# Edge attention on a graph: clip and exps for two batches at once, messages a round later, and more column tiles

## The chip, the cores and the metric

The kernel runs on one core of one Trainium2 chip. The metric is the device time of one execution in microseconds. Engines are named as the profile names them: PE (TensorE: matmuls, and PEld for its weight loads), DVE (VectorE), ACT (ScalarE), POOL (GpSimd), SP (SyncE, which issues DMAs here).

## What is computed

A graph has N = 6250 nodes of 128 features and E = 206250 edges, sorted by the node they end in. Heads H = 8 of width 16. Cut to what matters:

```python
Qh, Kh, Vh = h @ WQ, h @ WK, h @ WV          # per node, as (N, 8, 16)
Eh = edge_attr @ WE                          # per edge
score = einsum('ehd,ehd,ehd->eh', Kh[src], Qh[dst], Eh) / sqrt(16)
score = exp(clip(score, -5, 5))
msg = Vh[src] * score[:, :, None]
wV, Z = segment_sum(msg, dst), segment_sum(score, dst)
out = layernorm(x + wV / (Z + 1e-6))
```

Each edge needs the K and V rows of its source node (a random node) and the Q row of its end node (neighbours in the sorted order).

## The kernel before, in words

**Tiles and batches.** 128 edges are a tile; there are 1612 tiles. A batch is four tiles (`B`), 401 of these, and five last ones of two or one tile (the last `TAIL` = 8 tiles), 406 batches in all. The main loop (L621) makes a round for each batch, plus three rounds that drain it.

**K and V rows.** For the first 12 batches (`XB`) POOL gathers rows of x itself and PE projects them (`project`, L440). Meanwhile `table` (L271) projects all nodes and writes the rows of K and V to a table in HBM. From batch 12 on, `gather` (L420) fetches rows of 256 numbers from that table with one indirect DMA for each tile (L429), issued by POOL, into one of `GB` = 12 buffers `kvrows`. In program order a gather stands `GLEAD` = 2 rounds ahead of its use, on POOL's own queue; from batch 18 on it also waits for the Q expansion of a batch `lag(b)` rounds back (L361: 12 rounds at first, one fewer every 40 batches, never under 3).

**Column tiles.** 163 batches have their fourth tile built without a gather: three batches in seven (`COLP = (7, 3)`), from batch 24 on. The columns of x for its 128 edges are copied one by one out of `xT_sb` into a tile `xcol`, at addresses that are loaded into registers first (L391). ACT copies `COLA` = 8 x 11 = 88 of them, one instruction each (L402); DVE copies `COLV` = 8 x 5 = 40, two to an instruction by an OR of two addresses (L399). "Runs" are eight columns with one register load: eight instructions on ACT, four on DVE. `columns` (L372) issues the runs that are due at a point of the round. PE then projects the tile (`project_columns`, L404, two rounds before the batch's turn), and ACT copies the result into the batch's `kvrows` (`place_columns`, L414).

**A round.** For batch b PE makes the edge projection `eps` and the expansion of Q rows `qps` (`stage_a`, L489). DVE multiplies for the batch before it, b - 1 (`stage_b`, L504): `kq` (L507), `kqe` (L510), the sum over each head `sc` (L513), the clip (L516). Then ACT takes the exp twice (`weigh`, L519): into the message tile (L523) and into `exp_p` in PSUM (L524). DVE makes the message of batch b - 2 (`messages`, L555), and PE adds batch b - 2 into its window of nodes with one matmul a tile against a one-hot matrix (`stage_c`, L562, `agg`). DVE builds the one-hot matrices for two batches at a time (`stage_0`, L462, and `stage_0t`, L474), so every other round. When a window of 16 tiles is complete, ACT copies it to one of `SUMS` = 9 buffers; `finish` (L541) adds windows to blocks of 256 nodes (`finps`), ACT copies these (`fin`, L550), and `layernorm` runs on DVE.

**What sets the order.** From batch 12 on the order on each engine is the program order (`manual_schedule`, L623). Each round of DVE is written out by hand (L653 to L673): kq, one-hot or column runs, `fill`, kqe, one-hot or column runs, `fill`, sc, message, column runs, `fill`, clip, `fill`. `fill` (L613) puts in one small instruction: a cast or difference of the next block of Q rows (`q_rows`, L302, whose matmul PE makes at the end of a round, L689), or one step of a layernorm. Column runs stand behind kq and kqe only in rounds without one-hots.

Of the kernel before, what the change touches and what calls it, by code (L numbers as in the profile page):

```python
# [9 lines left out]
F32 = mybir.dt.float32  # L10
# [4 lines left out]
ALU = mybir.AluOpType  # L15
AX = mybir.AxisListType

P = 128
N, E, D, H, DH = 6250, 206250, 128, 8, 16
NT = (E + P - 1) // P  # L20
EPAD = NT * P
B = 4
# [5 lines left out]
MW = D + H  # L28
# [8 lines left out]
LAST = NT - TAIL  # L37
# [12 lines left out]
QLOOK = 3  # L50
QREG = 16
COL0 = 24
COLP = (7, 3)
COLA = (8, 11)
COLV = (8, 5)
COLL = 8
RING = 4096
XCOLS = 4
SUMS = 9
XT_AT = RING + P  # L60
NB = (N + P - 1) // P

# [40 lines left out]
def edge_attention(ctx: ExitStack, tc: tile.TileContext, x, xT, srcT, srcC, dstT, dstB, dst0, bnd, lo, eaT,  # L103
                   wq, wkv, we, out, kv, qtab, qs, relD):
    nc = tc.nc
# [26 lines left out]
    batches = cut_batches()  # L132
# [8 lines left out]
    with ExitStack() as fast:  # L141
# [105 lines left out]
        psX = fast.enter_context(tc.tile_pool(name="psX", bufs=1, space=bass.MemoryType.PSUM))  # L247

        iota_p = psX.tile([P, HW], F32, name="iota_p")
        exp_p = psX.tile([P, B, H], F32, name="exp_p")  # L250
        nc.vector.tensor_copy(iota_p, iota_f[:, :HW])

        def pair_bank(i, name, shape):
# [88 lines left out]
            nc.sync.dma_start(rels[c][:, :n], relD.rearrange("j e -> (j e)")[None, c * RC * P:c * RC * P + n]  # L342
                              .to_broadcast([QROWS, n]))

        chunks, aggs, sums, st8, expanded = {}, {}, {}, {}, {}

        def load_chunk(c):
            if c in chunks or c * CH >= NT:
# [20 lines left out]

        addresses, fetched = {}, {}  # L370

        def columns(eng, b, share=1.0):  # L372

            size, runs = COLA if eng is nc.scalar else COLV
            first = 0 if eng is nc.scalar else COLA[0] * COLA[1]
            engine = mybir.EngineType.Activation if eng is nc.scalar else mybir.EngineType.DVE
            copy = eng.copy if eng is nc.scalar else eng.tensor_copy
            due = int((b - COL0 + COLL - 1 + share) * runs * COLP[1] / COLP[0] + 1e-6)
            total = len(col_batches) * runs
            while copied.get(engine, 0) < min(due, total):  # L380
                k, j = divmod(copied.get(engine, 0), runs)
                copied[engine] = copied.get(engine, 0) + 1
                if k not in col_tiles:
                    col_tiles[k] = wp.tile([P, P], F32, name="xcol", bufs=XCOLS)
                to, j = col_tiles[k].bitcast(U8), first + j * size
                known = addresses.setdefault(engine, [])
                while len(known) < 2 and fetched.get(engine, 0) < total:
                    kf, jf = divmod(fetched.get(engine, 0), runs)
                    fetched[engine] = fetched.get(engine, 0) + 1
                    jf = first + jf * size  # L390
                    known.append(nc.values_load_multi_w_load_instructions(  # L391
                        col_at[kf % col_half:kf % col_half + 1, kf // col_half, jf:jf + size], engines=(engine,),
                        min_val=XT_AT, max_val=XT_AT + 8 * (N - 1) + 4,
                        skip_runtime_bounds_check_because="edges name nodes")[1])
                at = known.pop(0)
                if eng is nc.vector:
                    for c in range(0, size, 2):
                        both = [xT_bytes[:, ds(a - XT_AT, 8)] for a in at[c:c + 2]]
                        eng.tensor_tensor(to[:, 4 * (j + c):4 * (j + c) + 8], *both, op=ALU.bitwise_or)  # L399
                    continue  # L400
                for c in range(size):
                    copy(to[:, 4 * (j + c):4 * (j + c) + 4], xT_bytes[:, ds(at[c] - XT_AT, 4)])  # L402
# [50 lines left out]

        def together(b):

            t0 = batches[b][0]
            n = len(batches[b])
            if n == B and b + 1 < nbat and len(batches[b + 1]) == B and t0 % (2 * B) == 0:
                return [b, b + 1]
            return [] if n == B and t0 % (2 * B) else [b]  # L460

        def stage_0(b):  # L462
            group = together(b)
# [40 lines left out]
        def stage_b(b):  # L504
            n, g, oh, pq, pe = st8[b]
            t0 = wp.tile([P, B, D], F32, name="kq", bufs=2)
            nc.vector.tensor_tensor(t0[:, :n], g[:, :n, :D], pq[:, :n], op=ALU.mult)  # L507
            yield
            t1 = wp.tile([P, B, D], F32, name="kqe", bufs=2)
            nc.vector.tensor_tensor(t1[:, :n], t0[:, :n], pe[:, :n], op=ALU.mult)  # L510
            yield
            sc = wp.tile([P, B, H], F32, name="sc")
            nc.vector.tensor_reduce(sc[:, :n], t1[:, :n].rearrange("p b (h d) -> p b h d", h=H),  # L513
                                    axis=AX.X, op=ALU.add)
            yield
            nc.vector.tensor_scalar(sc[:, :n], sc[:, :n], -20.0, 20.0, op0=ALU.max, op1=ALU.min)  # L516
            st8[b] = [n, g, oh, sc]

        def weigh(b):  # L519

            n, g, oh, sc = st8[b]
            m = wp.tile([P, B, MW], F32, name="msg")
            nc.scalar.activation(m[:, :n, D:], sc[:, :n], AF.Exp, scale=0.25)  # L523
            nc.scalar.activation(exp_p[:, :n], sc[:, :n], AF.Exp, scale=0.25)  # L524
            st8[b] = [n, g, oh, m]

        def windows(q):

# [24 lines left out]
            blocks_out.append(copied_out)  # L553

        def messages(b):  # L555
            n, g, oh, m = st8[b]
            nc.vector.tensor_tensor(  # L557
                m[:, :n, :D].rearrange("p b (h d) -> p b h d", h=H),
                g[:, :n, D:].rearrange("p b (h d) -> p b h d", h=H),
                exp_p[:, :n, :, None].to_broadcast([P, n, H, DH]), op=ALU.mult)  # L560

        def stage_c(b):  # L562
            n, g, oh, m = st8.pop(b)
            for i in range(n):
                t = batches[b][i]
                k, _ = window_of(t)
                q = t * N // NT // P
                if q % 2 == 0 and q < NB and q not in loaded_x:
                    loaded_x.add(q)
                    xbs[q] = load_x(nc, sp, x, q, min(2, NB - q))  # L570
                final = k == NT
                if k not in aggs:
                    aggs[k] = psA.tile([P, 1, MW], F32, name="agg")
                    if final:
                        add_windows(aggs[k][:, 0], QL, True, False)
                tail = t == NT - 1 or window_of(t + 1)[0] != k
                nc.tensor.matmul(aggs[k][:, 0], oh[0][:, oh[1] + i * P:oh[1] + i * P + P], m[:, i, :],  # L577
                                 start=not final and t % (QUAD * G) == 0, stop=tail)
                if tail and final:
                    norms.insert(0, layernorm(nc, sp, aggs.pop(k), xbs.pop(QL), out, QL, 1, stores))  # L580
                elif tail:
                    sums[k] = sp.tile([P, MW], F32, name="sum", bufs=SUMS)
                    nc.scalar.copy(sums[k], aggs.pop(k)[:, 0])
                    while len(finished) < QL // 2 and all(v <= k for v, _ in windows(2 * len(finished) + 1)):
                        ready.append(len(finished))
                        finished.append(k)
# [23 lines left out]
        nc.vector.tensor_scalar(col_at, col_at, 8, XT_AT + 4, op0=ALU.mult, op1=ALU.add)  # L610
        second = col_at[:, :, COLA[0] * COLA[1]:].rearrange("p h (c s) -> p h c s", s=2)[:, :, :, 1]
        nc.vector.tensor_scalar(second, second, 4, None, op0=ALU.subtract)
        def fill():  # L613

            if qwork:
                build_q(0, False)
            elif norms and (not late or late.pop()) and next(norms[0], None) is None:
                norms.pop(0)

        held, late = [], []  # L620
        for b in range(nbat + 3):  # L621
            if b >= XB and not manual:
                manual.append(fast.enter_context(tc.manual_schedule()))  # L623
            held += [(b + SLAG, store) for store in stores]
# [29 lines left out]
            next(steps, None)  # L654
            if b + AHEAD < nbat and together(b + AHEAD):
                stage_0(b + AHEAD)
            elif b < nbat:
                columns(nc.vector, b, 0.5)
            fill()
            next(steps, None)  # L660
            if b + AHEAD < nbat and together(b + AHEAD):
                stage_0t(b + AHEAD)
            elif b < nbat:
                columns(nc.vector, b, 1.0)
            fill()
            next(steps, None)
            if 0 <= b - 2 < nbat:
                messages(b - 2)
            if b < nbat:
                columns(nc.vector, b)  # L670
            fill()
            next(steps, None)
            fill()  # L673
# [4 lines left out]
                blocks_out.pop(0)()  # L678
            if b < nbat:
                columns(nc.scalar, b)  # L680
            if 0 <= b - 2 < nbat:
                stage_c(b - 2)
            if b < nbat:
                project_columns(b + GLEAD)
                build_q(q_built(min(NJ - 1, batches[b][0] // WT + QLOOK + 2)), True)
                if not qwork and len(built) < q_built(
                        min(NJ - 1, batches[min(nbat - 1, b + 3)][0] // WT + QLOOK + 2)):
                    qwork.append(q_rows(len(built)))
                    next(qwork[0])  # L689
            if b == min(60, nbat):  # L690
                count_inside()
            if b == min(80, nbat + 1):
# [160 lines left out]
```

## Time and profile before

| | |
|---|---|
| median of 3 runs | 1854.44 us (1854.39 to 1854.63) |
| profiled execution | 1852.51 us, span of its profile 1850.7 us |
| mean granted TensorE clock | 0.918 |
| DMA | 378.38 MB, mean 204 GB/s |
| HBM read, written | 360.30 MB, 14.81 MB |

Times are microseconds, unless marked ns. In a group's row stand the line, the engine, the operation, the tiles written and read, the count, then the busy time and the mean ns of one instruction, then the idle time of the engine just before them and who ended most of it. "issue" is time in which an engine waited for nothing that the profile shows. In a table of stretches each engine has its busy time and, in brackets, the number of its instructions; behind them stand the granted clock, the DMA share and GB/s. In a table of waits stand the waiter, who released it, total us, times, and the longest. In the order of time a row has the start, the length and the count of the instructions merged. An instruction's length runs to its last write, and the next one of the engine starts before that, so what an instruction takes of its engine is read from start to start.

### The profile page before, as it was taken

To read this page: it belongs to the slowest core of one execution; us is meant where nothing else is said; L and a number is where in the kernel's file an instruction comes from. 1 tells how busy PE (TensorE), PEld (TensorE's weight loads), DVE (VectorE), ACT (ScalarE), POOL (GpSimd) and SP (SyncE) were. 2 spreads that over 40 slices of the span, in tenths; PEclk is the share of its full clock that TensorE was granted. 3 is DMA by queue.
4 is the path that set the end of the run, shared out by engine and by line. 5 is a ranking of instruction groups with operands and counts; after the bars stand their busy time and mean duration, and the time that the engine had idled before them with its cause. 6 is when DMAs were issued, how large, how long until landed. Compare 5 with 4: busy or idle time off the path is not lost.

```text
span 1850.7 us, 47948 instructions
## 1 busy us (share of the span) xinstructions
PE 1306.9 (71%) x9104; PEld 1134.8 (61%) x9104; DVE 1655.5 (89%) x6514; ACT 1626.7 (88%) x15519; POOL 1385.6 (75%) x1456
## 2 busy tenths in 40 slices
PE   6887767667677676667776676766766677667666
PEld 4776656566566565566665565655666667656555
DVE  5579999999998999999998898989998899898987
ACT  2439899899999999999999899999899899999983
POOL 6777777777777777777777777777777777777774
PEclk7998899899998989999899998999898988898998
DMA  9776667767766776767767677667776686667762
GB/s 283 231 230 194 195 204 230 204 184 213 223 192 192 221 207 200 225 196 208 216 196 207 188 204 220 195 187 224 209 207 182 194 236 187 197 188 229 216 190 76
DMA packets 171226, 378.38 MB, mean 204 GB/s; under 512 B 58622, under 2 KB 84556, under 8 KB 170918
## 3 DMA queue, kind: packets, MB, share of 16 engines
q0 software_dynamic: 68768, 186.80, 35.1%
q1 hardware_dynamic: 101010, 187.38, 33.9%
q14 instruction: 234, 1.92, 0.3%
q8 instruction: 74, 1.21, 0.3%
q10 hardware_dynamic: 1140, 1.06, 0.2%
HBM read 360.30 MB, written 14.81 MB: 203 GB/s over the span
## 4 chain that ended last, share of the span: by engine, by line
DVE 38%; DMA 15%; PE 14%; ACT 12%; issue 8%; POOL 6%; DVEq 4%; ACTq 2%; SPq 0%; POOLq 0%
DMA kvrows<-kv,src 13%; ACT xcol L402 10%; DVE xcol L399 7%; DVE kqe L510 7%; DVE kq L507 6%; POOL kvrows L429 6%; DVE sc L513 6%; PE eps L497 5%; DVEq L391 4%; PE agg L577 4%; DVE msg L557 3%; DVE onehot L469 3%; DVE onehotT L482 2%; ACTq L391 2%; PE kvps L451 1%
## 5 line engine op out<-in xcount | busy, mean ns | idle before, releaser
L429 POOL DMA_INDIRECT kvrows<-kv,src x1401 | 1338.0, 955 | 427.4 <-issue 318.7
L402 ACT COPY xcol<-xT_sb 128x4 uint8 x14344 | 1447.0, 191 | 52.1 <-issue 45.3
L497 PE MATMUL eps<-we_sb,ea 128*128 128x128 f32 x3224 | 499.6, 303 | 416.4 <-DVE kqe L510 243.7
L497 PEld LDWEIGHTS eps<-we_sb,ea 128*128 128x128 f32 x3224 | 435.3, 209 | 510.5 <-issue 351.4
L577 PE MATMUL agg<-msg,onehot 128*128 128x136 f32 x3224 | 533.2, 313 | 89.5 <-DVE msg L557 82.8
L577 PEld LDWEIGHTS agg<-msg,onehot 128*128 128x128 f32 x3224 | 454.4, 211 | 142.2 <-DVE msg L557 126.8
L507 DVE TENSOR_TENSOR kq<-kvrows,qps 128x512 f32<-128x512 f32 x406 | 275.7, 679 | 82.6 <-DMA kvrows<-kv,src 33.8
L399 DVE TENSOR_TENSOR xcol<-xT_sb 128x8 uint8 x3260 | 312.9, 162 | 26.8 <-issue 21.1
L557 DVE TENSOR_TENSOR msg<-kvrows,exp_p 128x512 f32<-128x512 f32 x406 | 273.1, 673 | 7.9 <-ACT exp_p L524 7.9
L510 DVE TENSOR_TENSOR kqe<-kq,eps 128x512 f32<-128x512 f32 x406 | 273.9, 675 | 3.0 <-PE eps L497 2.6
L513 DVE TENSOR_REDUCE sc<-kqe 128x32 f32<-128x512 f32 x406 | 272.2, 670 | 0.7
L500 PE MATMUL qps<-qw,onehotT 126*128 126x128 bf16 x1612 | 169.5, 230 | 0.0
L523 ACT ACTIVATE msg<-sc 128x32 f32<-128x32 f32 x406 | 92.5, 228 | 78.9 <-DVE sc L516 65.3
L500 PEld LDWEIGHTS <-onehotT 126*128 126x128 bf16 x1612 | 135.0, 104 | 8.6
L469 DVE TENSOR_TENSOR onehot<-iota_p,dst_sb 128x512 f32<-128x512 f32 (+2 forms) x206 | 138.2, 672 | 2.0 <-PE agg L577 2.0
L411 PE MATMUL colkv<-wkv_sb,xcol 128*128 128x256 f32 x326 | 108.0, 416 | 0.0
L482 DVE TENSOR_SCALAR onehotT<-relb,node 126x1024 bf16<-126x1024 bf16 (+2 forms) x206 | 102.7, 499 | 3.3 <-DMA relb<-relD 1.8
L516 DVE TENSOR_SCALAR sc<-sc 128x32 f32<-128x32 f32 x406 | 81.2, 200 | 0.3
L524 ACT ACTIVATE exp_p<-sc 128x32 f32<-128x32 f32 x406 | 73.6, 181 | 0.0
L429 POOL DMA_INDIRECT kvrows<-x,src x48 | 46.6, 971 | 20.5 <-issue 11.6
L418 ACT COPY kvrows<-colkv 128x256 f32<-128x256 f32 x163 | 58.9, 361 | 1.4 <-PE colkv L411 1.3
L411 PEld LDWEIGHTS colkv<-wkv_sb,xcol 128*128 128x128 f32 x326 | 56.9, 215 | 0.0
(76 smaller groups left out, 536.3 us busy)
## 6 DMA issues: line engine op xcount, KB each, us to landing
ea<-eaT SPq DMA_DIRECT2D x201, 512.0 KB
relb<-relD SPq DMA_DIRECT2D x100, 504.0 KB
kvrows<-kv,src POOLq DMA_INDIRECT x1401
qw<-qs SPq DMA_DIRECT2D x202, 31.5 KB
kv<-kvst SPq DMA_DIRECT2D x12, 512.0 KB
qs<-qst SPq DMA_DIRECT2D x48, 96.0 KB
xst<-xT SPq DMA_DIRECT2D x12, 256.0 KB
xb<-x SPq DMA_DIRECT2D x24, 128.0 KB
```

Source lines behind the costliest of these rows:

```text
L399: eng.tensor_tensor(to[:, 4 * (j + c):4 * (j + c) + 8], *both, op=ALU.bitwise_or)
L402: copy(to[:, 4 * (j + c):4 * (j + c) + 4], xT_bytes[:, ds(at[c] - XT_AT, 4)])
L411: nc.tensor.matmul(pk, col_tiles.pop(k), wkv_sb, start=True, stop=True)
L429: ins = nc.gpsimd.indirect_dma_start(out=g[:k, i, :f], out_offset=None, in_=rows, in_offset=bass.IndirectOffsetOnAxis(ap=src_col(t)[:k], a ...
L469: nc.vector.tensor_tensor(tl[:, HW:].rearrange("p (t n) -> p t n", n=P)[:, :n, :HW], iota_p[:, None, :].to_broadcast([P, n, HW]), rel[:, t ...
L497: nc.tensor.matmul(pe[:, i, :], ea[:, i * P:i * P + P], we_sb, start=True, stop=True)
L500: expanded[b] = nc.tensor.matmul(pq[:, i, :], ohT[:, i * P:i * P + P], loaded[t0 // WT], start=True, stop=True)
L507: nc.vector.tensor_tensor(t0[:, :n], g[:, :n, :D], pq[:, :n], op=ALU.mult)
L510: nc.vector.tensor_tensor(t1[:, :n], t0[:, :n], pe[:, :n], op=ALU.mult)
L513: nc.vector.tensor_reduce(sc[:, :n], t1[:, :n].rearrange("p b (h d) -> p b h d", h=H), axis=AX.X, op=ALU.add)
L557: nc.vector.tensor_tensor(m[:, :n, :D].rearrange("p b (h d) -> p b h d", h=H), g[:, :n, D:].rearrange("p b (h d) -> p b h d", h=H), exp_p[ ...
L577: nc.tensor.matmul(aggs[k][:, 0], oh[0][:, oh[1] + i * P:oh[1] + i * P + P], m[:, i, :], start=not final and t % (QUAD * G) == 0, stop=tail)
```

## The change

- `COLP` goes to (13, 6): six batches in 13 have a column tile. `COLA` is 8 x 10, `COLV` 8 x 6: ACT copies 80 columns of a tile, DVE 48. `SUMS` goes to 8.
- `columns` takes a bound `most`. DVE calls it at three places in every round with a bound of one run: behind kq (and a one-hot), behind kqe (and a one-hot), and behind the message. Before, it stood behind kq and kqe only in rounds without one-hots, and behind the message with no bound.
- Batches are paired (`together`, `group_of`): `sc`, the message tile and `exp_p` hold two batches. The sum over heads of each batch writes its half; the clip comes once, with the second; `weigh` takes both exps once, for the pair.
- `messages` and `stage_c` come for batch b - 3 in round b, where they came for b - 2; the loop has one round more.
- `fresh`: after the matmul of a block of Q rows, three calls of `fill` are counted down, the third of which makes the first cast.

```diff
-COLP = (7, 3)
-COLA = (8, 11)
-COLV = (8, 5)
+COLP = (13, 6)
+COLA = (8, 10)
+COLV = (8, 6)
...
-SUMS = 9
+SUMS = 8
...
-        exp_p = psX.tile([P, B, H], F32, name="exp_p")
+        exp_p = psX.tile([P, 2 * B, H], F32, name="exp_p")
...
-        def columns(eng, b, share=1.0):
+        def columns(eng, b, share=1.0, most=99):
...
-            while copied.get(engine, 0) < min(due, total):
+            while copied.get(engine, 0) < min(due, total) and most:
+                most -= 1
...
-            t0 = batches[b][0]
-            n = len(batches[b])
-            if n == B and b + 1 < nbat and len(batches[b + 1]) == B and t0 % (2 * B) == 0:
-                return [b, b + 1]
-            return [] if n == B and t0 % (2 * B) else [b]
+            first = LAST // B
+            if (b - first if b >= first else b) % 2:
+                return []
+            return [i for i in (b, b + 1) if i < nbat and (i < first) == (b < first)]
+
+        def group_of(b):
+
+            return together(b) or together(b - 1)
...
-            sc = wp.tile([P, B, H], F32, name="sc")
-            nc.vector.tensor_reduce(sc[:, :n], t1[:, :n].rearrange("p b (h d) -> p b h d", h=H),
+            group = group_of(b)
+            if b == group[0]:
+                scores[b] = wp.tile([P, 2 * B, H], F32, name="sc", bufs=2)
+            sc, k = scores[group[0]], sum(len(batches[i]) for i in group if i < b)
+            nc.vector.tensor_reduce(sc[:, k:k + n], t1[:, :n].rearrange("p b (h d) -> p b h d", h=H),
                                     axis=AX.X, op=ALU.add)
+            st8[b] = [n, g, oh, k]
             yield
-            nc.vector.tensor_scalar(sc[:, :n], sc[:, :n], -20.0, 20.0, op0=ALU.max, op1=ALU.min)
-            st8[b] = [n, g, oh, sc]
+            if b == group[-1]:
+                nc.vector.tensor_scalar(sc[:, :k + n], sc[:, :k + n], -20.0, 20.0, op0=ALU.max, op1=ALU.min)
 
         def weigh(b):
 
-            n, g, oh, sc = st8[b]
-            m = wp.tile([P, B, MW], F32, name="msg")
+            group = group_of(b)
+            if b != group[-1]:
+                return
+            sc, n = scores.pop(group[0]), sum(len(batches[i]) for i in group)
+            m = wp.tile([P, 2 * B, MW], F32, name="msg", bufs=2)
             nc.scalar.activation(m[:, :n, D:], sc[:, :n], AF.Exp, scale=0.25)
             nc.scalar.activation(exp_p[:, :n], sc[:, :n], AF.Exp, scale=0.25)
-            st8[b] = [n, g, oh, m]
+            for i in group:
+                st8[i].append(m)
...
+        fresh = []
+
         def fill():
 
-            if qwork:
+            if fresh:
+                fresh.pop()
+            if qwork and not fresh:
                 build_q(0, False)
...
-        for b in range(nbat + 3):
+        for b in range(nbat + 4):
...
                 stage_0(b + AHEAD)
-            elif b < nbat:
-                columns(nc.vector, b, 0.5)
+            if b < nbat:
+                columns(nc.vector, b, 1.0, 1)
...
                 stage_0t(b + AHEAD)
-            elif b < nbat:
-                columns(nc.vector, b, 1.0)
+            if b < nbat:
+                columns(nc.vector, b, 1.0, 1)
...
-            if 0 <= b - 2 < nbat:
-                messages(b - 2)
+            if 0 <= b - 3 < nbat:
+                messages(b - 3)
             if b < nbat:
-                columns(nc.vector, b)
+                columns(nc.vector, b, 1.0, 1)
...
-            if 0 <= b - 2 < nbat:
-                stage_c(b - 2)
+            if 0 <= b - 3 < nbat:
+                stage_c(b - 3)
...
                     next(qwork[0])
+                    fresh[:] = [0, 0, 0]
```

More of the change, by code (lines that the diff above doesn't have):

```diff
@@ L343, in load_rel @@
                               .to_broadcast([QROWS, n]))
-        chunks, aggs, sums, st8, expanded = {}, {}, {}, {}, {}
+        chunks, aggs, sums, st8, expanded, scores = {}, {}, {}, {}, {}, {}
         def load_chunk(c):
@@ L555, in messages @@
         def messages(b):
-            n, g, oh, m = st8[b]
+            n, g, oh, k, m = st8[b]
             nc.vector.tensor_tensor(
-                m[:, :n, :D].rearrange("p b (h d) -> p b h d", h=H),
+                m[:, k:k + n, :D].rearrange("p b (h d) -> p b h d", h=H),
                 g[:, :n, D:].rearrange("p b (h d) -> p b h d", h=H),
-                exp_p[:, :n, :, None].to_broadcast([P, n, H, DH]), op=ALU.mult)
+                exp_p[:, k:k + n, :, None].to_broadcast([P, n, H, DH]), op=ALU.mult)
         def stage_c(b):
-            n, g, oh, m = st8.pop(b)
+            n, g, oh, at, m = st8.pop(b)
             for i in range(n):
@@ L576, in stage_c @@
                 tail = t == NT - 1 or window_of(t + 1)[0] != k
-                nc.tensor.matmul(aggs[k][:, 0], oh[0][:, oh[1] + i * P:oh[1] + i * P + P], m[:, i, :],
+                nc.tensor.matmul(aggs[k][:, 0], oh[0][:, oh[1] + i * P:oh[1] + i * P + P], m[:, at + i, :],
                                  start=not final and t % (QUAD * G) == 0, stop=tail)
```

## The prediction

> **What bounds the kernel now.** I read the engine totals first, then the costliest groups, then the gathers alone in the order of time.
>
> ```profile
> PE 1306.9 (71%) x9104; PEld 1134.8 (61%) x9104; DVE 1655.5 (89%) x6514; ACT 1626.7 (88%) x15519; POOL 1385.6 (75%) x1456
> L429 POOL DMA_INDIRECT kvrows<-kv,src x1401 | 1338.0, 955 | 427.4 <-issue 318.7
> L429 POOL DMA_INDIRECT kvrows<-x,src x48 | 46.6, 971 | 20.5 <-issue 11.6
> ```
>
> ```profile
> 3.76 1.11 POOL L429 DMA_INDIRECT kvrows<-x,src  x1 [2.19 <-DMA src<-srcT]
> ...
> 1819.43 0.95 POOL L429 DMA_INDIRECT kvrows<-kv,src  x1 [0.30 <-issue]
> ...
> 1833.18 0.90 POOL L429 DMA_INDIRECT kvrows<-kv,src  x1 [0.31 <-PE agg L577]
> ```
>
> DVE and ACT look like the bounds at 89% and 88%, POOL like a spare engine at 75%. The order of time says otherwise. 1819.43 to 1833.18 is 11 gathers: 1.25 us each, 0.95 busy and 0.30 that comes with every gather. From the first to the last, 1448 steps take 1829.4 us, 1.263 each: 1810 us is cadence, only 19 us anything else. POOL issues gathers from end to end, so the end is fixed by their number, as long as the computing keeps up.
>
> ```profile
> 70.00:130.00 60.00, 45.43 (x48) 1.00 0.64 201
> ...
> 332.60:846.00 513.40, 389.10 (x409) 0.94 0.71 207
> 846.00:1740.00 894.00, 677.16 (x711) 0.91 0.71 205
> ```
>
> ```profile
> 0.00:332.60 332.60, 40.98 (x60) 0.90 0.73 221
> 332.60:846.00 513.40, 81.93 (x121) 0.94 0.71 207
> ```
>
> ```profile
> 332.60:846.00 513.40, 363.20 (x2642) 316.12 (x2642) 485.09 (x1966) 491.24 (x4816) 389.10 (x409) 0.94 0.71 207
> 846.00:1740.00 894.00, 627.05 (x4402) 549.10 (x4400) 808.35 (x3273) 832.72 (x8084) 677.16 (x711) 0.91 0.71 205
> ```
>
> The first fence is the gathers alone by stage, the second the kq products (one a round), the third all engines (PE, PEld, DVE, ACT, POOL). In 332.6 to 846 there are 120 rounds of 4.28 us, while POOL needs 4 - 3/7 = 3.571 gathers a round at 1.254, 4.48 us. Computing is faster there and eats up the lead of the gathers; DVE idles 513.4 - 485.1 = 28.3 us. After 846 DVE idles 86 of 894 us and its longest wait is for gathered rows:
>
> ```profile
> DVE kq L507 <- DMA kvrows<-kv,src: 30.8, 24, 3.5
> ```
>
> So two paths race: POOL's count, and the rounds of DVE. POOL's wins now.
>
> **The change, part by part.** *Gathers.* Column tiles go from 163 to 176 (382 x 6 // 13; the change's words say 175), so 13 gathers go: 13 x 1.25 = **-16.3 us** on POOL's path.
>
> *DVE's column work.* COLV goes from 20 to 24 instructions a tile: 20 x 163 = 3260 becomes 24 x 176 = 4224. In the 120 rounds above, the built order has 333 runs of four where 257 stood.
>
> ```profile
> 902.98 0.68 DVE L510 TENSOR_TENSOR kqe<-kq,eps 128x512 f32<-128x512 f32 x1
> 903.58 0.48 DVE L482 TENSOR_SCALAR onehotT<-relb,node 126x1024 bf16<-126x1024 bf16 x1
> ...
> 905.78 0.18 DVE L516 TENSOR_SCALAR sc<-sc 128x32 f32<-128x32 f32 x1
> 905.87 0.67 DVE L507 TENSOR_TENSOR kq<-kvrows,qps 128x512 f32<-128x512 f32 x1
> 906.47 0.38 DVE L399 TENSOR_TENSOR xcol<-xT_sb 128x8 uint8 x4
> 906.78 0.68 DVE L510 TENSOR_TENSOR kqe<-kq,eps 128x512 f32<-128x512 f32 x1
> ```
>
> From start to start, a run takes 906.78 - 906.47 = 0.31 us, a long product 0.60, a clip 0.09. So 76 more runs cost 76 x 0.31 = +23.6 us.
>
> *Clips.* 60 of 120 go: -60 x 0.09 = -5.4. The other 60 have 64 elements, a form the trace lacks: between nothing and another 0.09 more each. The nearest rows are
>
> ```profile
> L516 DVE TENSOR_SCALAR sc<-sc 128x32 f32<-128x32 f32 x120 | 24.1, 201 | 0.0
> L785 DVE TENSOR_SCALAR rz<-fin 128x16 f32<-128x16 f32 x7 | 1.2, 175 | 5.5 <-ACT fin L550 5.5
> ```
>
> 16 elements more took 26 ns, so 32 more take some 0.05: +3. DVE's busy time becomes 485.1 + 23.6 - 2.4 = 506.3 us (ends 503.6 and 508.7).
>
> *DVE's waits*, the same stage:
>
> ```profile
> DVE xcol L399 <- issue: 8.2, 24, 0.8
> DVE kq L507 <- PE qps L500: 5.8, 10, 0.8
> DVE rz L785 <- ACT fin L550: 5.5, 7, 1.5
> DVE qst L309 <- PE qrows L305: 5.2, 12, 1.2
> ```
>
> "issue" before xcol is the register load that each run needs:
>
> ```profile
> L391 DVEq TENSOR_LOAD <-col_at x815: 591/606/1614, 130.1 to 1812.1; - x163
> ```
>
> 0.61 us doesn't fit behind another run (0.31) but fits behind a long instruction and a run (0.91). Runs now stand behind each other after the messages; the new order puts one behind each of three long spots. I take 8.2 to 2. The countdown of three fills puts the first q cast behind the messages, not 0.6 us behind its matmul: 5.2 to 0. The wait for qps falls in rounds with few runs between kqe and the next kq (none: 0.60 + 0.60 + 0.09 of cover); now two runs stand there in nearly every round: 5.8 to 3. The wait for fin stays. With 28.3 - 24.7 = 3.6 of small ones, 14 us of idle is left (ends: 4 and 28.3).
>
> 506.3 + 14.1 = 520.4 us for 120 rounds, **4.337 a round**; POOL will need 4 - 6/13 = 3.538 gathers at 1.254, **4.437**. DVE still has 0.10 us a round in hand.
>
> *Messages and sums a round later.* The gather buffers (12) come free a round later, when one more message product has run. Early that bites:
>
> ```profile
> 0.00:114.10 114.10, 6.86 (x10) 0.90 0.82 256
> ...
> 0.00:341.20 341.20, 41.29 (x61) 0.89 0.73 220
> ```
>
> ```profile
> 0.00:114.10 114.10, 80.76 (x84) 0.90 0.82 256
> 0.00:341.20 341.20, 253.31 (x264) 0.89 0.73 220
> ```
>
> ```profile
> 115.81 0.67 DVE L557 TENSOR_TENSOR msg<-kvrows,exp_p 128x512 f32<-128x512 f32 x1
> ```
>
> (msg on DVE, gathers on POOL, both counted from 0.) At 114.1 POOL has started 84 gathers, 21 batches, and goes on with batch 21, in the buffer of batch 9, whose message (the tenth) has run. In the new order that message stands where the eleventh stood, ending at 116.5: POOL waits **+2.4 us**, for good. Near 341 (batch 71) the margin is about nothing again, POOL by then some 2 us quicker and DVE some 2 slower: **+1.6**, ends 0 and 6. Behind the waiting gather stand only later gathers, 30 us ahead of use there.
>
> *ACT.* Its copies fall from 88 x 163 = 14344 to 80 x 176 = 14080, its exps from 812 to 408.
>
> ```profile
> 902.75 0.23 ACT L523 ACTIVATE msg<-sc 128x32 f32<-128x32 f32 x1
> 902.88 0.18 ACT L524 ACTIVATE exp_p<-sc 128x32 f32<-128x32 f32 x1
> 903.00 1.14 ACT L402 COPY xcol<-xT_sb 128x4 uint8 x11
> ```
>
> A copy takes 0.10 us, the exps 0.25 a batch: 264 x 0.10 = 26 us less, and 202 x 0.25 = 51 us less if an exp of 64 elements cost no more than one of 32, nothing if it cost double. I take half. None of it is on a path that ends last; ACT gets slack. It now waits for a clip once in two rounds; queued behind its exps are column copies and the placing of projected columns, read by kq two rounds later. The message of a pair's first batch follows the clip by a round, as now, so no DVE wait is added. exp_p has one buffer: the next pair's exp waits for the message that reads it last, but that message stands ahead of the clip which the exp awaits anyway.
>
> *Edits at nothing:* PE's 13 column projections (PE 71% busy) and sums a round later; eight sum buffers (a block needs about six); stores and loads of x that move a few places on SP past loads of edges and q rows issued four to six rounds ahead. The q store waits half a round (2.2 us) longer and holds SP's later loads, against 17 us of lead. Without such a cover each would cost DVE a wait of that length in one round of eight.
>
> *The end.*
>
> ```profile
> 1826.06 0.69 DVE L507 TENSOR_TENSOR kq<-kvrows,qps 128x512 f32<-128x512 f32 x1
> ...
> 1838.35 0.29 DVE L507 TENSOR_TENSOR kq<-kvrows,qps 128x128 f32<-128x128 f32 x1
> ...
> 1839.96 0.29 DVE L557 TENSOR_TENSOR msg<-kvrows,exp_p 128x128 f32<-128x128 f32 x1 [0.32 <-ACT exp_p L524]
> ```
>
> One more round after the last kq holds one message: **+0.5** (ends 0 and 1.6, the stretch from last kq to last message).
>
> **Sum.** -16.3 + 2.4 + 1.6 + 0.5 = -11.8. The profiled execution took 1852.5 (span 1850.7), so 1840.7; the median of the runs stands 1.9 above it: **1842.6 us**.
>
> Does DVE stay inside? The kq of batch 400, the last of four tiles and 340 rounds after 332.6, is at 1826.1 now and by POOL's path at 1826.1 - 16.3 + 4.0 = 1813.8. By DVE's, with 2.4 us lost before 332.6: 335 + 340 x 4.337 = 1809.6. POOL decides by 4 us. DVE takes over above (1813.8 - 335)/340 = 4.349 a round, 15.6 us of idle left in the 120 rounds; above 4.386 (20.0 us left of 28.3) there is no gain.
>
> **Rivals.**
> *A, slower: DVE saturates.* Place: the rounds from 332.6 on. If the waits come back elsewhere (PE late, runs late) and all 28.3 us stay, a round takes (506.3 + 28.3)/120 = 4.455: batch 400 at 335 + 340 x 4.455 = 1849.7, 23.6 later than now: **1878**. It makes the kernel slower from 20 us of idle on. For it: DVE would be 95% busy, and every wait then ends last. Against it: 13 of the 28 us are register loads and q casts, which the new order moves.
> *B, between:* 15.6 to 20 us stay: **1844 to 1855**.
> *C, buffers bind:* POOL waits 10 us instead of 4 in the first 70 rounds: **1849**. For it: margins of nothing at two places; against: DVE gains 0.2 us a round on POOL now (4.28 against 4.48) and 0.1 by my sum, so the margin grows.
> *D, POOL slows under DVE.* The gathers kept 60.0/48 = 1.250 us without any column run (70 to 130) and 1.255 beside them (332.6 to 846): in proportion, 30% more runs cost 0.0015 x 1436 = 2 us. But if each of the 964 added instructions held POOL for its 0.0775 us (0.31/4), 75 us: **1917**. The Trainium skill, SBUF — State Buffer, section Who interferes with whom, speaks for D: a DVE instruction with two SBUF inputs, as these are, contends with a GpSimd instruction that reads SBUF. The 1.250 against 1.255 says that the gathers hardly meet it.
> *E, the waits go but the clips and exps gain nothing:* the 64-element forms cost double; DVE's sum is 2.4 us higher, within B.
>
> **How the numbers follow.** Forecast 0.60 (1838 to 1848); A 0.19; B and E 0.12; C 0.07; D 0.02. Measurement tells 0.2%, 3.7 us, from no change. Faster: 0.60 + half of B + C = 0.70; within 0.2%: 0.11, from B and the near end of A; slower 0.19. The range 1837 to 1866 leaves out D and the upper half of A, and a little below.
>
> **What will show it.** 1436 gathers, still 1.25 us from start to start, none waiting after the first 80 rounds; POOL's last near 1821. DVE between 332.6 and 846 at 97% busy, "issue" before xcol and the q cast's wait nearly gone. Lead of gathers over kq shrinking by 0.1 us a round, so waits for gathered rows only in the last quarter, where 30.8 us stood. A clip row of x204, mean some 250 ns. I am wrong if POOL shows gaps over 0.3 us throughout (DVE leads: A) or if its cadence rises (D).

## The result, and the profile after

The changed kernel took 1847.21 us in the median (1844.41 to 1848.53, seven runs), the kernel before 1854.44 (1849.36 to 1858.05, seven runs): ratio 0.9955, 95% interval 0.9941 to 0.9969. It is faster by 0.45%, 7 us by the medians and 8 by the ratio, inside the range and less than the 11.8 us forecast. Ratios here and below are taken over the fast runs alone, which leaves out four of the six runs with 13 buffers on a slower chip and no other. The profiled execution took 1847.3 us, with a span of 1845.5 (1852.5 and 1850.7 before).

The page of the changed kernel: engine totals and the gathers.

```profile
span 1845.5 us, 48388 instructions
PE 1297.4 (70%) x9130; PEld 1115.6 (60%) x9130; DVE 1705.4 (92%) x7272; ACT 1586.4 (86%) x14864; POOL 1377.2 (75%) x1443
L430 POOL DMA_INDIRECT kvrows<-kv,src x1388 | 1330.1, 958 | 426.1 <-issue 306.1
```

The totals tell little: DVE has 50 us more to do, POOL 8 us less, and the span falls by 5.2. The order of time on POOL says where it ends:

```profile
3.60 1.11 POOL L430 DMA_INDIRECT kvrows<-x,src  x1 [2.03 <-DMA src<-srcT]
...
67.08 1.13 POOL L430 DMA_INDIRECT kvrows<-x,src  x1 [0.30 <-issue]
68.52 0.94 POOL L430 DMA_INDIRECT kvrows<-x,src  x1 [0.31 <-issue]
72.66 0.94 POOL L430 DMA_INDIRECT kvrows<-kv,src  x1 [3.19 <-DVE msg L569]
...
1823.53 0.95 POOL L430 DMA_INDIRECT kvrows<-kv,src  x1 [0.30 <-PE qps L504]
1824.78 0.90 POOL L430 DMA_INDIRECT kvrows<-kv,src  x1 [0.30 <-PE agg L589]
```

Still 1.25 us from gather to gather at the end, and the last one comes 8.4 us earlier (1824.78 against 1833.18). Thirteen gathers fewer should have made that 16.3. At 72.66 stands one part of what is missing: the first gather of batch 12 waits 3.19 us for a message of DVE.

The stretches of the changed kernel, all engines, and then its kq products on DVE:

```profile
332.60:846.00 513.40, 365.68 (x2615) 316.43 (x2616) 496.70 (x2186) 473.74 (x4553) 389.25 (x408) 0.93 0.68 204
846.00:1740.00 894.00, 624.91 (x4475) 541.62 (x4474) 846.24 (x3715) 821.62 (x7835) 677.92 (x709) 0.94 0.71 205
```

```profile
332.60:846.00 513.40, 80.71 (x119) 0.93 0.68 204
```

DVE is at 97% between 332.6 and 846, 119 rounds in 513.4 us, 4.31 to 4.35 a round. Its waits in that stretch:

```profile
DVE kq L511 <- PE qps L504: 6.3, 11, 0.9
DVE rz L802 <- ACT fin L562: 5.6, 7, 2.1
DVE xcol L400 <- issue: 0.4, 2, 0.2
```

The waits for register loads fell from 8.2 us to 0.4, those for the q cast from 5.2 to none. The wait for qps stayed. Behind that stretch, from 846 to 1740, DVE's longest wait is for gathered rows again, as before the change:

```profile
DVE kq L511 <- DMA kvrows<-kv,src: 15.9, 15, 2.7
```

So there DVE is held by POOL again and again. The kq products of that stretch, before the change and after it:

```profile
846.00:1740.00 894.00, 136.64 (x201) 0.91 0.71 205
846.00:1740.00 894.00, 138.01 (x203) 0.94 0.71 205
```

Taken from the first start of a kq to the last, a round takes 4.48 us before and 4.42 after, close to what the gathers of a round need at 1.254 us each (4.48 and 4.44).

Where the span went, taken from the starts of all gathers in the two traces (what each stretch took beyond 1.25 us a gather):

| | before | after | difference |
|---|---|---|---|
| gathers counted at 1.25 us | 1448 steps | 1435 steps | -16.3 |
| beyond it, first 40 gathers | 5.3 | 6.0 | +0.7 |
| gathers 40 to 60 (batch 12) | 0.1 | 3.2 | +3.1 |
| gathers 60 to 280 | 3.3 | 5.7 | +2.4 |
| gather 280 to the last | 10.8 | 12.6 | +1.8 |
| start of the first gather | 3.8 | 3.6 | -0.2 |
| from the last gather to the end | 17.5 | 20.7 | +3.2 |
| sum | | | -5.3 |

### The profile page after: what moved, and what is told of

Read it like the earlier page. It is cut to its first block, busy times and chain, and to the rows that moved or that the text cites. A ratio compares the mean times of both kernels' runs of the same rounds, so it can differ in the third digit from the quotient of the medians.

```text
span 1845.5 us, 48388 instructions
## 1 busy us (share of the span) xinstructions
PE 1297.4 (70%) x9130; PEld 1115.6 (60%) x9130; DVE 1705.4 (92%) x7272; ACT 1586.4 (86%) x14864; POOL 1377.2 (75%) x1443
## 4 chain that ended last, share of the span: by engine, by line
DVE 43%; PE 15%; DMA 12%; ACT 11%; issue 8%; DVEq 4%; POOL 4%; ACTq 1%; SPq 0%; POOLq 0%
DMA kvrows<-kv,src 10%; ACT xcol L403 9%; DVE xcol L400 8%; DVE kqe L514 7%; DVE kq L511 7%; PE eps L501 6%; DVE sc L520 5%; DVE msg L569 4%; POOL kvrows L430 4%; DVEq L392 4%; PE agg L589 4%; DVE onehot L473 3%; DVE onehotT L486 3%; PE finps L548 2%; ACTq L392 1%
## 5 line engine op out<-in xcount | busy, mean ns | idle before, releaser
L403 ACT COPY xcol<-xT_sb 128x4 uint8 x14080 | 1429.7, 190 | 61.0 <-issue 53.5
L501 PE MATMUL eps<-we_sb,ea 128*128 128x128 f32 x3224 | 488.0, 298 | 391.3 <-DVE kqe L514 194.6
L501 PEld LDWEIGHTS eps<-we_sb,ea 128*128 128x128 f32 x3224 | 422.9, 204 | 490.0 <-issue 358.7
L589 PEld LDWEIGHTS agg<-msg,onehot 128*128 128x128 f32 x3224 | 443.9, 207 | 173.4 <-DVE msg L569 170.0
L400 DVE TENSOR_TENSOR xcol<-xT_sb 128x8 uint8 x4224 | 417.7, 157 | 10.7 <-issue 6.2
L511 DVE TENSOR_TENSOR kq<-kvrows,qps 128x512 f32<-128x512 f32 x406 | 274.2, 675 | 56.2 <-DMA kvrows<-kv,src 20.7
L473 DVE TENSOR_TENSOR onehot<-iota_p,dst_sb 128x512 f32<-128x512 f32 (+1 forms) x204 | 137.2, 673 | 2.1 <-PE agg L589 2.1
L534 ACT ACTIVATE msg<-sc 128x64 f32<-128x64 f32 (+1 forms) x204 | 51.9, 254 | 82.7 <-DVE sc L525 70.6
L486 DVE TENSOR_SCALAR onehotT<-relb,node 126x1024 bf16<-126x1024 bf16 (+1 forms) x204 | 99.0, 486 | 6.3 <-DMA relb<-relD 4.3
L548 PE MATMUL finps<-sum,shift 128*128 128x136 f32 x370 | 53.2, 301 | 0.0
L548 PEld LDWEIGHTS finps<-sum,shift 128*128 128x128 f32 x370 | 49.8, 209 | 0.0
```

Source lines behind the costliest of these rows:

```text
L473: nc.vector.tensor_tensor(tl[:, HW:].rearrange("p (t n) -> p t n", n=P)[:, :n, :HW], iota_p[:, None, :].to_broadcast([P, n, HW]), rel[:, t ...
L501: nc.tensor.matmul(pe[:, i, :], ea[:, i * P:i * P + P], we_sb, start=True, stop=True)
```

## The experiments

Theory 1 is the forecast's: POOL's count of gathers sets the end, and what it waits comes on top. Theory 2: DVE's work sets the end, and the saved clips pay for the columns. The twelve runs fell on five chips. On two of them the kernel before took 1853 and 1854 us, on the other three 2488 to 2537; ratios are always against the kernel before on the same chip, and the runs of the slower chips are told apart, below, because POOL's count doesn't set the end there. Each trace is of one execution, and executions of one kernel on one of the two faster chips differ by up to 7 us, so a difference of 1 or 2 us between two traces shows nothing by itself.

### Fewer columns

```diff
-COLP = (13, 6)
+COLP = (7, 3)
```

in the changed kernel: 163 column tiles again, less work on DVE and ACT, 13 gathers more on POOL.

> The changed kernel with 163 column tiles instead of 176, for a chip where the kernel before takes about 1854 us. DVE has 13 x 24 column instructions less than in the full change (some 25 us), POOL 13 gathers more (16 us). Theory 1: POOL's path is back at 1449 gathers, with the longer tail: ratio 1.001 to 1.005, last gather at 1836 to 1842 us. Theory 2: DVE's path is 25 us shorter than in the full change: ratio 0.980 to 0.988.

Measured: 1857.96 us against 1853.94, ratio 1.0027 (1.0013 to 1.0042). That is inside what theory 1 expected. Less work on DVE and ACT made the kernel slower than the full change, by nearly what 13 gathers take (16.3 us): 1.0027 - 0.9955 is 0.0072, 13 us. The end of POOL's order of time in this run:

```profile
1838.88 0.95 POOL L430 DMA_INDIRECT kvrows<-kv,src  x1 [0.30 <-issue]
1840.13 0.90 POOL L430 DMA_INDIRECT kvrows<-kv,src  x1 [0.31 <-PE eps L501]
```

1840.13 against 1824.78: 15.4 us (the execution profiled here was 3.7 us above the median of its runs). From 846 to 1740 a round is back at 4.48 us. Theory 2 falls on this chip. The run also prices everything else in the change without the 13 gathers: a loss of 0.3%.

### Thirteen gather buffers

```diff
-GB = 12
+GB = 13
-EB = 5
+EB = 4
-load_chunk(batches[b][0] // CH + EB - 3)
+load_chunk(batches[b][0] // CH + EB - 2)
```

in the changed kernel.

> The changed kernel with 13 gather buffers instead of 12 (four edge buffers instead of five, loaded as far ahead as before, make room), for a chip where the kernel before takes about 1854 us. Theory 1 (POOL's count sets the end, and the later release of gather buffers cost POOL some 6 us in the first quarter): these waits go, the last gather comes 4 to 6 us earlier, near 1820 us, ratio 0.993. Theory 2 (DVE's work sets the end): buffers change nothing, ratio 0.995 to 0.996.

Measured: 1843.57 us against 1853.94, ratio 0.9950 (0.9936 to 0.9964). POOL at batch 12 and at the end:

```profile
68.80 0.94 POOL L430 DMA_INDIRECT kvrows<-x,src  x1 [0.30 <-issue]
70.04 0.95 POOL L430 DMA_INDIRECT kvrows<-kv,src  x1 [0.30 <-issue]
```

```profile
1817.95 0.94 POOL L430 DMA_INDIRECT kvrows<-kv,src  x1 [0.40 <-PE qps L504]
1820.73 0.90 POOL L430 DMA_INDIRECT kvrows<-kv,src  x1 [1.83 <-PE qps L504]
```

The wait at batch 12 is gone, and the last gather comes 4.1 us earlier than in the changed kernel, near the 1820 expected: the buffers' part is shown, 3 us at batch 12. The ratio expected, 0.993, lies just outside the interval, and the intervals of this kernel and the changed one overlap: they can't be told apart by time. Some of the gain went into a new wait: the last gathers shown wait for the Q expansion three rounds back (qps), 1.6 us beyond the usual 0.30.

### The columns alone

The kernel before, with `COLP`, `COLA`, `COLV`, the three calls of `columns` with a bound of one run and `fresh` as changed, and with clip, exps, messages and sums as before, batch by batch, b - 2.

> The columns' part alone for the third time, for a chip where the kernel before takes about 1854 us. Theory 1 (POOL's count of gathers sets the end; the later release of gather buffers and the longer tail take back part of the gain): ratio 0.991 to 0.993, about 1840 us, last gather near 1818 us, no long wait of POOL at batch 12, tail behind the last gather as before (17.5 us). Theory 2 (DVE's work sets the end, and the saved clips and exps pay for the columns): ratio 0.997 to 1.005, POOL waiting all along.

Measured: 1844.63 us against 1852.67, ratio 0.9949 (0.9933 to 0.9966): no different from the full change. Theory 1 expected 0.991 to 0.993, a last gather near 1818 and a tail of 17.5 us behind it, so it missed too. Its last gathers (the profiled execution, 1849.45 us, was the slowest of four, 4.8 above the median), with 19.0 us behind the last:

```profile
1827.44 0.95 POOL L430 DMA_INDIRECT kvrows<-kv,src  x1 [0.30 <-PE agg L578]
1828.69 0.90 POOL L430 DMA_INDIRECT kvrows<-kv,src  x1 [0.30 <-issue]
```

The long wait at batch 12 is indeed nearly gone:

```profile
70.76 0.94 POOL L430 DMA_INDIRECT kvrows<-kv,src  x1 [0.70 <-DVE msg L558]
```

But between gathers 60 and 280 POOL loses 9.9 us beyond 1.25 a gather, where the full change loses 5.7 and the kernel before 3.3, and 14.3 after that (12.6 and 10.8). Of the 9.9, 5.2 are waits for buffers: at batches 50, 51, 53, 71 and 72 a gather is late and starts 0.7 to 0.8 us behind the end of the message whose buffer it takes. For batch 71 that is the message of batch 59:

```profile
345.25 0.68 DVE L558 TENSOR_TENSOR msg<-kvrows,exp_p 128x512 f32<-128x512 f32 x1
```

```profile
346.66 0.94 POOL L430 DMA_INDIRECT kvrows<-kv,src  x1 [3.22 <-PE eps L498]
```

Two things made DVE late there. Its rounds are longer without the saved clips: 4.36 us from kq to kq between 332.6 and 846, against 4.31 in the full change. And at 219 us it waited once for a load:

```profile
DVE wq L192 <- DMA dB_sb<-dstB: 4.1, 1, 4.1
```

The trace of the full change has no such wait, but it isn't the pairs that spare it: the run with fewer columns has the pairs, waits 5.4 us for the same load, and then 4.6 us for buffers at batches 48 to 71. So while POOL is as far ahead as its buffers allow, a late DVE costs POOL time. That the pairs give back time in this way, and take it at batch 12, fits the two traces but isn't shown; by the measured times, what the pairs add to the columns can't be told from nothing.

### On the slower chips

Nine runs fell where the kernel before takes 2488 to 2537 us. They were meant for the questions above:

> The columns' part of the change alone: 176 column tiles, 80 and 48 columns, one run behind each long spot, the countdown before the q cast; clip, exps, messages and sums as before, batch by batch and a round earlier. Theory 1 (POOL's count of gathers sets the end, and the later release of gather buffers and the longer tail take back part of the gain): 13 gathers fewer without the early waits and the longer tail, so 13 to 16 us under the kernel before, ratio 0.992, last gather near 1818 us, faster than the full change (0.9955). Theory 2 (DVE's work sets the end, and the saved clips and exps pay for the columns): DVE has 203 clips more to do than in the full change and ACT 202 pairs of exps, so it is slower than the full change, ratio 0.997 to 1.005, with waits of POOL beyond the 0.30 us of each gather.

> The columns' part alone once more, to be compared on a chip where the kernel before takes about 1854 us. Theory 1 (POOL's count of gathers sets the end; the later release of gather buffers and the longer tail take back part of the gain): ratio 0.991 to 0.993, about 1840 us, last gather near 1818 us, no long wait of POOL at batch 12. Theory 2 (DVE's work sets the end, and the saved clips and exps pay for the columns): ratio 0.997 to 1.005, POOL waiting all along.

> The pairs alone: clip and both exps for two batches at once, messages and sums a round later, eight sum buffers; 163 column tiles, their sizes, their spots and the q cast as before. Theory 1: 1449 gathers as before, plus the early waits of POOL for buffers (4 to 6 us) and a tail that is longer by 1 to 3 us: slower than before by 5 to 9 us, ratio 1.003 to 1.005. Theory 2 (DVE's work sets the end): 200 clips fewer are some 20 us less on DVE, so faster by 5 to 15 us, ratio 0.992 to 0.997.

> The pairs alone (clip and exps for two batches at once, messages and sums a round later; 163 column tiles of 88 and 40, at their old spots), for a chip where the kernel before takes about 1854 us. Theory 1: 1449 gathers, plus POOL's wait at batch 12 (3 us) and a tail longer by 2 to 3 us: ratio 1.002 to 1.004. Theory 2: DVE has 200 clips less, some 20 us: ratio 0.989 to 0.995.

> The changed kernel with three batches in seven as column batches again (163 column tiles instead of 176), everything else as changed. DVE has 13 x 24 column instructions less, ACT 13 x 80 copies less, POOL 13 gathers more. Theory 1: 16 us slower than the full change, about 1863 us where before takes 1854: ratio 1.004 to 1.006. Theory 2: DVE has some 25 us less to do, so faster than the full change, ratio 0.985 to 0.993.

> The changed kernel with every paired clip made twice (204 clips of 0.11 us more on DVE, 0.06 us a round; the second changes nothing). Theory 1: DVE has about 0.1 us a round in hand against POOL, so nothing is lost: within 2 us of the full change, ratio 0.995 to 0.997. Theory 2: DVE's 22 us come on top, 0.8 to 1.2% slower than the full change, ratio 1.003 to 1.008.

> The changed kernel with every paired clip made twice (204 more clips of 64 elements, 0.11 us each, 22 us of DVE in all; the second changes nothing), for a chip where the kernel before takes about 1854 us. Theory 1 (POOL's count sets the end): DVE goes at 4.32 us a round until it is held by gathers and POOL at 4.43, so 0.055 us a round more on DVE is free but for some more waiting for buffers early: ratio 0.995 to 0.998. Theory 2 (DVE sets the end): 22 us more, ratio 1.006 to 1.008.

> The changed kernel with 13 gather buffers instead of 12 (and four edge buffers instead of five, loaded as far ahead as before, to make room). A gather then waits for the same round as before the change. Theory 1: the waits of POOL in the first 70 rounds that the change added (3 us at batch 12, some 2 more until batch 70) go, so the last gather is 4 to 6 us earlier, near 1820 us, and the time 1841 to 1843: ratio 0.993. Theory 2: DVE sets the end, buffers change nothing: ratio 0.995 to 0.996.

> The changed kernel with 13 gather buffers (and four edge buffers) and column tiles from batch 18 on instead of 24: 179 column tiles, 1433 gathers. Theory 1 (POOL's count sets the end): three gathers fewer than with 13 buffers alone, 3.75 us, if POOL does not wait more for buffers: last gather near 1817 us, ratio 0.992 to 0.9945. Theory 2 (DVE sets the end): 72 column instructions more, 6 us: slower than with 13 buffers alone, ratio 0.996 to 0.999. A chip where the kernel before takes 2490 us would tell nothing of either.

Their edits, where not shown above: the pairs alone are the changed kernel with

```diff
-COLP = (13, 6)
-COLA = (8, 10)
-COLV = (8, 6)
+COLP = (7, 3)
+COLA = (8, 11)
+COLV = (8, 5)
```

and with column runs at their old spots, without `fresh`; the double clip puts `for _ in range(2):` ahead of the paired clip; the last one has `COL0 = 18` beside the 13 buffers.

| kernel | ACT's column copies | pairs | ratio on the same chip (95%) |
|---|---|---|---|
| columns alone | 14080 | no | 0.9877 (0.9847 to 0.9907), again 0.9875 (0.9835 to 0.9915) |
| changed, fewer columns | 13040 | yes | 0.9824 (0.9790 to 0.9859) |
| changed, 13 buffers | 14080 | yes | 0.9849 (0.9785 to 0.9913), from two runs |
| changed, double clip | 14080 | yes | 1.0003 (0.9982 to 1.0024), again 1.0059 (1.0028 to 1.0090) |
| changed, 13 buffers, from batch 18 | 14320 | yes | 1.0022 (0.9986 to 1.0057) |
| pairs alone | 14344 | yes | 1.0174 (1.0136 to 1.0212), again 1.0224 (1.0180 to 1.0268) |

The groups and the totals of the columns alone on such a chip say why neither theory can be tried there:

```profile
PE 1589.6 (64%) x9130; PEld 1393.4 (56%) x9130; DVE 1766.5 (71%) x7478; ACT 1686.2 (68%) x15268; POOL 1370.9 (55%) x1443
L430 POOL DMA_INDIRECT kvrows<-kv,src x1388 | 1324.1, 954 | 1075.8 <-issue 453.2 <-PE qps L501 344.9 <-remote 88.1
L403 ACT COPY xcol<-xT_sb 128x4 uint8 x14080 | 1502.8, 190 | 581.5 <-issue 569.9 <-DVE qst L309 1.0
```

The same kernel on the chip where it took 1844.63 us has for these rows

```profile
PE 1304.7 (71%) x9130; PEld 1123.3 (61%) x9130; DVE 1720.8 (93%) x7478; ACT 1608.6 (87%) x15268; POOL 1377.7 (75%) x1443
L403 ACT COPY xcol<-xT_sb 128x4 uint8 x14080 | 1421.7, 190 | 63.2 <-issue 56.0
```

and the granted clock of TensorE, the last number of a core's row, is lower on the slow chip:

```profile
core 0: 2497.8 us, clock 0.773
```

```profile
core 0: 1847.7 us, clock 0.926
```

PE is busy 285 us longer there for the same 9130 matmuls, and yet no engine is over 71% busy: the span grew by 650 us, DVE's work by 46 and ACT's by 78. A gather takes 954 ns, 959 on the other chip, but POOL stands idle 1076 us ahead of its gathers (429 there). ACT stands idle 582 us ahead of its column copies, 570 of it in "issue", where the profile shows nothing that it waited for (56 on the other chip). In the order of time, in the middle of a run:

```profile
1210.75 0.38 ACT L403 COPY xcol<-xT_sb 128x4 uint8 x3 [0.19 <-issue]
1211.51 0.19 ACT L403 COPY xcol<-xT_sb 128x4 uint8 x1 [0.38 <-issue]
1212.23 0.29 ACT L403 COPY xcol<-xT_sb 128x4 uint8 x2 [0.52 <-issue]
1213.64 0.48 ACT L403 COPY xcol<-xT_sb 128x4 uint8 x4 [1.12 <-issue]
```

Copies that elsewhere follow each other by 0.10 us come in ones to fours, with holes of 0.2 to 1.1 us between. The chain that ended last is mostly ACT in this run:

```profile
ACT 48%; issue 24%; PE 8%; DVE 8%; ACTq 6%; another core or an unknown queue 3%; DMA 2%; POOL 1%; DVEq 1%; SPq 0%; POOLq 0%
```

So a third path leads there, ACT's, and POOL's count doesn't set the end. Two things follow, and no more. The halves of the change work against each other: columns alone gain 1.2%, pairs alone lose 1.7 to 2.2%. And on the kernels with pairs the time doesn't go with the gathers: fewer columns, slower elsewhere, is the fastest here. It is the one with the fewest of ACT's copies (13040), but the copies alone don't order the others: 24 copies are between the last two rows, which stand 1.5 to 2% apart and differ in the buffers and in the spots and sizes of the column runs as well. The changed kernel itself was not run on such a chip. What makes ACT stand in "issue" there, whether the lower clock of TensorE is its cause or comes with it, and by which step the pairs cost time, stay open: no run tells it. The kernel with columns from batch 18 ran on such a chip alone, so whether it beats the others where POOL leads is not known either. The pairs alone and the double clip, meant to try how much DVE has in hand, ran on such chips alone too: where POOL leads, DVE's margin is read from traces, and no run there puts work on DVE and nothing else.

## Why the prediction was right, and which terms were off

The mechanism held where it was made for: POOL's count sets the end (fewer columns: +15.4 us at the last gather), DVE stays just inside, and the sign follows. The gain forecast was too large by 4.6 us in the medians (1842.6 forecast, 1847.2 measured) and by 6.6 in the profiled execution (1840.7 and 1847.3); the 2 us between lie in which executions were profiled. The time alone doesn't speak for the forecast: 1847 lies in the ranges of the forecast and of B, and near C. The rounds of DVE, the waits for buffers and the run with fewer columns tell them apart. Two terms were mis-sized, the end and the cadence, which stood at nothing. By the steps:

*Gathers, -16.3.* 1436 gathers (1388 and 48), 1.25 us from start to start: right.

*DVE's work and waits.* Forecast 506.3 us busy and 14.1 idle for 120 rounds, 4.337 a round; measured 496.7 and 16.7 for 119, and 4.31 from kq to kq. The waits for register loads and q casts went as said; the wait for qps was to fall to 3 us and stayed at 6.3. The paired clip was mis-sized:

```profile
L525 DVE TENSOR_SCALAR sc<-sc 128x64 f32<-128x64 f32 x59 | 12.2, 207 | 0.0
```

207 ns, 6 more than at 32 elements, where I took 50 more from a row with other operands. The paired exps on ACT took 254 and 208 ns against 228 and 181. Neither decided. The waits for gathered rows were to come only in the last quarter; but for two early ones they came from 1035 on, 8.4 us of them before 1400.

*Messages a round later, +4.0.* The kind was right; the size was 3.0, and the places were wrong. A gather that is held by its buffer starts 0.3 to 0.8 us behind the end of the message that frees it. By that sign POOL waits 2.9 us at batch 12 and 0.1 at batch 21, where I had 2.4; near batch 71, where I had 1.6, it doesn't wait at all. So the +2.4 between gathers 60 and 280 belong to the cadence, below. I had moved each message to the spot of the next one. In the changed kernel

```profile
70.02 0.20 DVE L525 TENSOR_SCALAR sc<-sc 128x64 f32<-128x64 f32 x1
71.11 0.69 DVE L511 TENSOR_TENSOR kq<-kvrows,qps 128x512 f32<-128x512 f32 x1 [0.89 <-ACT kvrows L453]
71.71 0.68 DVE L569 TENSOR_TENSOR msg<-kvrows,exp_p 128x512 f32<-128x512 f32 x1
```

the first message (71.71) comes behind the first clip of a pair (70.02), which needs both batches, and behind the third kq; before, it stood behind the second kq, and the next message 2.6 us on:

```profile
66.61 0.68 DVE L557 TENSOR_TENSOR msg<-kvrows,exp_p 128x512 f32<-128x512 f32 x1
...
69.23 0.69 DVE L557 TENSOR_TENSOR msg<-kvrows,exp_p 128x512 f32<-128x512 f32 x1 [0.39 <-ACT exp_p L524]
```

So it is 5.1 us later, not 2.6, and POOL waits at batch 12, not first at batch 21. The 13 buffers show that this wait is the buffer's.

*Cadence, at nothing.* Under rival D I worked out 2 us for gathers a little slower beside more column work, and left it out of the sum. After gather 60, waits for buffers aside, the changed kernel lost 18.2 us beyond 1.25 a gather, the kernel before 14.1: +4.1. With 163 column tiles the two traces have 14.1 and 14.9, with 176 the three have 15.3 to 19.0 (the wait for qps at the end of the run with 13 buffers taken off). So it may go with the column tiles; whether the gathers themselves are slower or short waits for DVE come in, no run separates. D in full, 75 us, did not come.

*The end, +0.5.* This step failed: +3.2. The order of time on DVE behind the last gather (1824.78):

```profile
1830.64 0.29 DVE L511 TENSOR_TENSOR kq<-kvrows,qps 128x128 f32<-128x128 f32 x1
...
1833.01 0.27 DVE L569 TENSOR_TENSOR msg<-kvrows,exp_p 128x128 f32<-128x128 f32 x1
...
1837.93 0.59 DVE L822 TENSOR_SCALAR h<-h,mv,y 128x128 f32<-128x128 f32 x2
```

The last kq stands 5.9 us behind the last gather (5.2 before), the last message 2.4 behind that (1.6), the last of DVE ends 5.5 us after the message starts, as before. That is 1.5 of the 3.2. The one message that I had priced at 0.5 is 0.75 of it, and comes with the pairs. The other 0.7 doesn't: with pairs and 163 column tiles the last kq stands 5.2 us behind the last gather, in the columns alone 6.6. DVE also waits 1.76 us for window sums ahead of that kq (1.69 with fewer columns), but with fewer columns the kq is no later for it. The last 1.7 lie behind DVE's last instruction: 7.0 us to the end of the span against 5.3. In the traces of all kernels with pairs and five edge buffers this stretch is 6.7 to 7.0 us, without pairs 5.2 or 5.3, with pairs and four edge buffers 5.4 to 5.7. Only the last store and closing instructions lie in it. In all traces of the first kind, and in none of the others, SP stands still for 1.2 to 1.4 us between two of its closing semaphore instructions (1842.75 to 1844.09 in the changed kernel); why stays open.

Rival A, DVE saturated, priced at 1878, did not come, but it was close: DVE was 97% busy, and its rounds took 4.31 us where it would have taken over from 4.349. Its idle time, 16.7 us, lies where B has it (15.6 to 20), but with 4.17 us of work a round, not the 4.22 of the sum, so POOL still led. C, 10 us of waiting for buffers, did not come: it was 3.0. Against the 6.5 us missed in the span, the end has 2.7, the cadence after gather 60 4.1, the first 40 gathers 0.7, and the buffers took 1.0 less than forecast.

## What to carry to other kernels

An engine that is 75% busy can set the end, if each of its instructions brings a fixed gap (here 0.30 us behind 0.95): count starts, not busy time. When such a queue leads, a saving is worth what it takes off that queue, and a step that frees its buffers later can be paid at once, where the queue runs as far ahead as its buffers allow (2.9 us at batch 12). Price a pairing by its first pair: the first member waits for the second (5.1 us, not 2.6). And where two parts of a change are measured together, try each: the columns alone (ratio 0.9949) can't be told from the whole (0.9955).

## What the runs showed of the hardware that was not expected

On three of five chips the kernel before took 2488 to 2537 us, on the other two 1853 and 1854. TensorE's granted clock was 0.76 to 0.80 there against 0.92 to 0.94, and ACT's copies were held up 535 to 674 us by nothing that the profile shows, while the gathers (951 to 956 ns against 955 to 959) and the copies themselves (190 to 193 ns against 190 and 191) kept their lengths. The changed kernel with fewer columns was 0.3% slower than the kernel before on one chip and 1.8% faster on another. A clip over twice the elements cost 6 ns more of 201.
